# Layer 0 of a two-layer graph attention block: v and combination by ordinary products, the full-size sets by seven products

## The chip, the core and the metric

The kernel runs on one core of a Trainium2 chip. The metric is the device time of one execution in microseconds (us); the time of a kernel is the median of several executions. The core has four engines that compute: TensorE (PE in the profile) multiplies matrices and writes its results to PSUM, which here serves as eight banks of 128 partitions by 512 fp32 values; VectorE (DVE), ScalarE (ACT) and GpSimd (POOL) work element by element. Each engine takes its instructions in a fixed order, and engines wait for each other by semaphores. All data are fp32 except the adjacency mask, which is one byte per entry.

## The reference, cut to what matters

The input x holds 64 graphs of 256 nodes with 512 features, and adj a mask of 256 by 256 for each graph. Two attention layers follow each other; layer 0 has 4 heads of 64 (inner width 256), layer 1 has 8 heads of 64 (inner width 512).

```python
# layer 0
h = max(layernorm(x), 0)
q, k, v = h @ Wq, h @ Wk, h @ Wv             # 512 -> 256 each
sim = where(adj, q @ k.T / 8, -max)          # per head, 256 x 256
x = x + (softmax(sim) @ v) @ Wo + bo         # 256 -> 512, the "combination"
# layer 1
h = max(layernorm(x), 0)
h = layernorm(h) * gamma + beta
q, k, v = split(h @ w_qkv.T)                 # 512 -> 512 each
sim = where(adj | eye, q @ k.T / 8, -1e9)
x = x + (softmax(sim) @ v) @ w_out.T + b_out
```

## The kernel before

A step works on two graphs (G = 2, 512 tokens), so there are 32 steps. Layer 0 of a later step runs interleaved with layer 1 of an earlier one. The order on TensorE is written by hand: each call is placed on a time line by `at(period, place, function, ...)`, and the calls are then made in the order of their places. The order on the other engines is chosen by a scheduler when the kernel is built.

A matrix product C = A B with both factors cut into 2 by 2 blocks can be done with seven block products instead of eight, if sums of blocks are formed first and the products are added up afterwards. The kernel does so for every projection and for both combinations. A set is the seven products of one such multiplication. Each factor is kept as seven blocks (`NB = 7`): the four of the matrix, of which one is overwritten, and the sums. `PRODUCT[n]` names the weight block and the activation block that product n multiplies.

```python
NB = 7
A_OF = {(0, 0): 0, (0, 1): 1, (1, 1): 2, (1, 0): 3}
B_OF = ((0, 4, 3), (1, 3, 1))
PRODUCT = {1: (0, 0), 2: (1, 1), 3: (6, 2), 4: (2, 6), 5: (3, 3), 6: (4, 4), 7: (5, 5)}

def act_sums(b):                       # on GpSimd; b is hT, oT0 or oT1
    eng = nc.gpsimd
    eng.tensor_tensor(b[:, 5], b[:, 2], b[:, 3], ALU.subtract)
    eng.tensor_tensor(b[:, 3], b[:, 3], b[:, 0], ALU.subtract)
    eng.tensor_tensor(b[:, 4], b[:, 2], b[:, 3], ALU.subtract)
    eng.tensor_tensor(b[:, 6], b[:, 1], b[:, 4], ALU.subtract)
```

The products of a set are made in the order 1, 6, 7, 5, 2, 4, 3. Products 2, 4 and 3 are accumulated into the PSUM banks of products 1, 7 and 5, once those have been read. The pool `ps_mm` has four banks. It serves the projections, the combinations, the transposes of h and the weighted sums. The scores and the transposes of the probabilities (`sc`) have four banks of their own.

```python
def project_v(s, lyr, n):              # layer 0: width 128, 28 matmuls a step
    ...
    for t in range(NIC):               # NIC = 2 blocks of 128 tokens
        for c in range(HC):            # HC = 2 blocks of 128 features
            nc.tensor.matmul(
                bank[:, t, :], st["hT"][:, ba, c, t * P:(t + 1) * P], w[:, wa, c, 2, :], ...)
    evacuate(n, bank, token_rows(st[f"v{lyr}"], width))

def combine(s, lyr, n):                # layer 0: one chunk, 14 matmuls a step
    ...
    for t in range(NIC):
        for c in range(chunks):
            nc.tensor.matmul(
                bank[:, t, :], st[f"oT{lyr}"][:, ba, c, t * P:(t + 1) * P], w[:, wa, c, :], ...)
    accumulate(n, bank, token_rows(st["xt"], HD), st["u"])
```

`evacuate` copies products 1 and 2 on ScalarE and adds the others on VectorE. `accumulate` copies product 1 to `u` on ScalarE, adds product 6 to `u` on VectorE (L297), adds `u` to two quarters of xt on GpSimd and, after product 5, to a third; the other products are added to xt on VectorE.

A score set is 16 half-height matmuls, then per 128 rows a masked minimum on VectorE (L403) and an exponential on ScalarE (L409); a reciprocal (L414) and the scaling of the probabilities follow, half on VectorE (L419), half on ScalarE (L421). `turn` transposes the probabilities on TensorE (L430) and copies them back on both engines (L434, L436). `weigh` multiplies by v (L448), and ScalarE copies the result to oT (L454). `norm1` takes the moments of xt and of its ReLU on VectorE, makes the power -0.5 on GpSimd (L206) and the row scale on VectorE (L207); ScalarE scales the rows (L213). `mask` makes the additive mask on GpSimd (L188, and for layer 1 L192).

The order in which one step is placed, cut to the calls that matter here (p = s - 2 for layer 0, p = s for layer 1):

```python
for c in range(NC):
    at(p, 3.03 + 0.03 * c, transpose_h, s, 0, c)
at_set(p, 3.5, 1.0, project_qk, s, 0, 0)
at_set(p, 4.5, 0.5, project_v, s, 0)
at(p, 4.5, scores, s, 0, 0)
...
at_set(p, 9.0, 0.5, combine, s, 0)     # 9.0 is 3.0 of a later period
for t in range(NT):
    at(p, 9.5 + 0.25 * t, norm1, s, t)
...
at(p, 3.0, scores, s, 1, 1)
at(p, 3.75, scores, s, 1, 3)
at(p, 4.499, weigh, s, 1, 3, False, True)
at_set(p, 5.0, 1.0, combine, s, 1)
```

Of the kernel before, what the change touches and what calls it, by code (L numbers as in the profile page):

```python
# [8 lines left out]
FP = mybir.dt.float32  # L9
U8 = mybir.dt.uint8  # L10
AF = mybir.ActivationFunctionType
ALU = mybir.AluOpType
# [7 lines left out]
def kernel(  # L20
# [16 lines left out]
    nc = tc.nc  # L37
    P = 128
# [43 lines left out]

    NB = 7
    A_OF = {(0, 0): 0, (0, 1): 1, (1, 1): 2, (1, 0): 3}
    B_OF = ((0, 4, 3), (1, 3, 1))
    PRODUCT = {1: (0, 0), 2: (1, 1), 3: (6, 2), 4: (2, 6), 5: (3, 3), 6: (4, 4), 7: (5, 5)}

    def weight_sums(eng, w):
# [4 lines left out]

    def act_sums(b):
        eng = nc.gpsimd
        eng.tensor_tensor(b[:, 5], b[:, 2], b[:, 3], ALU.subtract)
        eng.tensor_tensor(b[:, 3], b[:, 3], b[:, 0], ALU.subtract)  # L97
        eng.tensor_tensor(b[:, 4], b[:, 2], b[:, 3], ALU.subtract)  # L98
        eng.tensor_tensor(b[:, 6], b[:, 1], b[:, 4], ALU.subtract)


    H0, H1, HD = I0 // 2, I1 // 2, D // 2
    HC, HP0, HP1 = NC // 2, PR0 // 2, PR1 // 2
    wqkv0 = const.tile([P, NB, HC, 3, H0], FP, name="wqkv0")
    wo0 = const.tile([P, NB, HP0, HD], FP, name="wo0")
    wqkv1 = const.tile([P, NB, HC, 3, H1], FP, name="wqkv1")
    wo1 = const.tile([P, NB, HP1, HD], FP, name="wo1")
    bo_b = const.tile([P, D], FP, name="bo_b")
# [2 lines left out]

    def first_weights():
        for (i, j), n in A_OF.items():
            for k, w in enumerate((wq, wk, wv)):
                nc.scalar.dma_start(
                    wqkv0[:, n, :, k, :],
                    w[j * D // 2:(j + 1) * D // 2, i * H0:(i + 1) * H0]
                    .rearrange("(c p) o -> p c o", p=P),
                )
        for (i, j), n in A_OF.items():  # L120
            nc.scalar.dma_start(
                wo0[:, n],
                wo[j * I0 // 2:(j + 1) * I0 // 2, i * HD:(i + 1) * HD]
                .rearrange("(c p) o -> p c o", p=P),
            )
        weight_sums(nc.vector, wqkv0)
        weight_sums(nc.gpsimd, wo0)
        for v, t in ((bo, bo_b), (b_out, bout_b)):
            nc.scalar.dma_start(t, bass.AP(tensor=v.tensor, offset=v.offset, ap=[[0, P], [1, D]]))

# [115 lines left out]
            row_scales(s, ve)  # L246


    def blocks_of(b, pairs):
        return b.rearrange("p n (c t) -> p n c t", c=pairs)  # L250

    def transpose_h(s, lyr, c):
        st = S[s]
        if c == 0:
            st["hT"] = act.tile([P, NB, HC, N], FP, name="hT")
        ph = ps_mm.tile([P, G, N], FP, name="mm")
        pv = ph.rearrange("p g n -> p (g n)")
        for t in range(NT):
            nc.tensor.transpose(pv[:, t * P:(t + 1) * P], st["h"][:, t, c * P:(c + 1) * P], ident)  # L259
        b0, b1, step = B_OF[c // HC]  # L260
        dst = st["hT"][:, b0:b1:step, c % HC, :]
        if lyr == 0:
            nc.scalar.activation(dst, ph, AF.Relu)
        else:
            nc.vector.tensor_scalar(
                dst, ph, gb[:, 0, c:c + 1], gb[:, 1, c:c + 1], op0=ALU.mult, op1=ALU.add
            )
        if c == NC - 1:
            act_sums(st["hT"])
# [50 lines left out]
    def project_qk(s, lyr, a, n):  # L320

        st = S[s]
        half, w = (PR0, PR1)[lyr] // 2, (wqkv0, wqkv1)[lyr]
        if n == 1:
            for pr in (a, a + half):
                st["qk", lyr, pr] = sm.tile([P, 2, T], FP, name="qk", bufs=3)
        t0, t1 = st["qk", lyr, a], st["qk", lyr, a + half]
        bank, first = bank_of(st, ("qk", a), n, N)
        wa, ba = PRODUCT[n]
        for k in range(2):  # L330
            for c in range(HC):
                nc.tensor.matmul(  # L332
                    bank[:, k, :], w[:, wa, c, k, a * P:(a + 1) * P], st["hT"][:, ba, c, :],
                    start=first and (k, c) == (0, 0), stop=(k, c) == (1, HC - 1),
                    skip_group_check=True,
                )
        evacuate(n, bank, (t0[:, :, :N], t0[:, :, N:], t1[:, :, :N], t1[:, :, N:]))
# [4 lines left out]
            for i in range(2) for j in range(2)  # L342
        ]

    def project_v(s, lyr, n):
        st = S[s]
        width, w = (H0, H1)[lyr], (wqkv0, wqkv1)[lyr]
        if n == 1:
            st[f"v{lyr}"] = act.tile([P, NT, 2 * width], FP, name=f"v{lyr}")
        bank, first = bank_of(st, "v", n, width)  # L350
        wa, ba = PRODUCT[n]
        for t in range(NIC):
            for c in range(HC):
                nc.tensor.matmul(  # L354
                    bank[:, t, :], st["hT"][:, ba, c, t * P:(t + 1) * P], w[:, wa, c, 2, :],
                    start=first and (t, c) == (0, 0), stop=(t, c) == (NIC - 1, HC - 1),
                    skip_group_check=True,
                )
        evacuate(n, bank, token_rows(st[f"v{lyr}"], width))

    def combine(s, lyr, n):
        st, chunks, w = S[s], (HP0, HP1)[lyr], (wo0, wo1)[lyr]
        if n == 1:
            st["u"] = sm.tile([P, NIC, HD], FP, name="u", bufs=1)
        bank, first = bank_of(st, "c", n, HD)
        wa, ba = PRODUCT[n]
        for t in range(NIC):
            for c in range(chunks):
                nc.tensor.matmul(  # L369
                    bank[:, t, :], st[f"oT{lyr}"][:, ba, c, t * P:(t + 1) * P], w[:, wa, c, :],  # L370
                    start=first and (t, c) == (0, 0), stop=(t, c) == (NIC - 1, chunks - 1),
                    skip_group_check=True,
                )
        accumulate(n, bank, token_rows(st["xt"], HD), st["u"])
# [62 lines left out]

    def weigh(s, lyr, pr, first, last):
        st, pT = S[s], S[s].pop(("pm", lyr, pr))
        half = (HP0, HP1)[lyr]  # L440
        if first:
            st[f"oT{lyr}"] = act.tile([P, NB, half, N], FP, name=f"oT{lyr}")
        po = ps_mm.tile([P, G, N], FP, name="mm")
        for g in range(G):
            for jc in range(NIC):
                for e in range(2):
# [3 lines left out]
                        st[f"v{lyr}"][:, g * NIC + jc, c0:c0 + DH],  # L450
                        pT[g, e][:, jc, :], start=(jc == 0), stop=(jc == NIC - 1),
                    )
        b0, b1, step = B_OF[pr // half]
        nc.scalar.copy(st[f"oT{lyr}"][:, b0:b1:step, pr % half, :], po)  # L454
        if last:
            act_sums(st[f"oT{lyr}"])

# [14 lines left out]
    for s in range(NSTEP):  # L474
# [7 lines left out]
        for c in range(NC):  # L482
            at(p, 3.03 + 0.03 * c, transpose_h, s, 0, c)
        at_set(p, 3.5, 1.0, project_qk, s, 0, 0)
        at_set(p, 4.5, 0.5, project_v, s, 0)
        at(p, 4.5, scores, s, 0, 0)
        at(p, 5.15, turn, s, 0, 0)
        at(p, 5.6, scores, s, 0, 1)
# [2 lines left out]
        at(p, 7.001, weigh, s, 0, 1, False, True)  # L491
        at(p, 7.4, load_x, s)
        at(p, 8.6, first_bias, s)
        at_set(p, 9.0, 0.5, combine, s, 0)
        for t in range(NT):
            at(p, 9.5 + 0.25 * t, norm1, s, t)
            at(p, 10.5 + 0.1 * t, scale_row, s, t)
# [3 lines left out]
            at(p, -0.85 + 0.15 * c, transpose_h, s, 1, c)  # L501
        at(p, 0.3, mask, s, 1)
        at_set(p, 0.0, 1.0, project_qk, s, 1, 0)
        at_set(p, 1.0, 1.0, project_v, s, 1)
        at_set(p, 2.0, 1.0, project_qk, s, 1, 1)
        at(p, 1.0, scores, s, 1, 0)
        at(p, 1.65, turn, s, 1, 0)
# [7 lines left out]
        at(p, 3.751, weigh, s, 1, 1, False, False)  # L515
        at(p, 4.25, turn, s, 1, 3)
        at(p, 4.499, weigh, s, 1, 3, False, True)
        at_set(p, 5.0, 1.0, combine, s, 1)
        at(p, 6.0, store, s)

    at(-3, 5.6, first_weights)
# [37 lines left out]
```

## Time and profile before

| what | value |
|---|---|
| time, median of 3 | 3909.32 us (3905.31 to 3909.89) |
| span of the profiled execution | 3907.4 us |
| TensorE busy | 3656.7 us, 94% |
| VectorE busy | 2410.3 us, 62% |
| ScalarE busy | 1940.0 us, 50% |
| GpSimd busy | 1379.9 us, 35% |
| HBM traffic | 29 GB/s over the span |
| distance of the layer-0 combinations of two steps that follow each other | 118.9 us |

The profile's page gives the busy time of each engine, the costliest groups of instructions (by source line, engine and tile) and the idle time before them with what ended it. The names are those of the program: `mm` is a bank of the pool `ps_mm`, `sc` a bank of the scores, `xt` the rows of x, `hT` and `oT` the transposed activations and attention outputs. Line numbers are those of the kernel before. An fp32 matmul appears as two matmul instructions, a transpose as one. The ends of matmuls are modelled, so the distance of starts is the surer measure. TensorE's loading of weights runs beside its matmuls.

### The profile page before, as it was taken

The numbers are of one execution on the slowest core, as the hardware profiler recorded it, in microseconds if no ns is written. First come the engines' busy times: TensorE is split into PE (matmuls) and PEld (weight loads), VectorE is DVE, ScalarE is ACT, GpSimd is POOL, SyncE is SP. The second block draws the span as 40 slices with busy tenths as digits, with TensorE's granted clock in tenths as the row PEclk, the third lists the DMA queues.
The fourth block names the chain that finished last, engine by engine and source line by source line (L and its number), as shares of the span: only waits on it lengthen the run. The fifth ranks groups of instructions, "written<-read, shape, count | busy, mean of one in ns | idle before, by whom it ended". The sixth has DMA issues, their size and how long they took to land. (4 is left out here: it accounts for less than half of the span.)

```text
span 3907.4 us, 59075 instructions
## 1 busy us (share of the span) xinstructions
PE 3656.7 (94%) x21953; PEld 3044.9 (78%) x21953; DVE 2410.3 (62%) x7001; ACT 1940.0 (50%) x5329; POOL 1379.9 (35%) x1170
## 2 busy tenths in 40 slices
PE   5999999999999999999999999999999999999988
PEld 4787778877777877778777878777787778787766
DVE  5566665666565666656665656666566656566654
ACT  3555554455554555544555455545455554554543
POOL 5234333343333343333433333433334333244331
PEclk9999999999999999999999999999999999999999
DMA  3011000110011110001100100100011001010000
GB/s 119 12 34 35 13 24 33 34 35 25 12 35 33 35 34 13 24 33 35 34 24 13 34 33 35 35 13 24 33 35 34 24 12 35 33 34 33 1 22 22
DMA packets 74128, 115.46 MB, mean 30 GB/s; under 512 B 18792, under 2 KB 22384, under 8 KB 73840
## 3 DMA queue, kind: packets, MB, share of 16 engines
q1 hardware_dynamic: 67584, 104.87, 8.1%
q10 hardware_dynamic: 6256, 6.82, 0.6%
q8 instruction: 172, 2.82, 0.3%
q14 instruction: 116, 0.95, 0.1%
HBM read 78.12 MB, written 33.55 MB: 29 GB/s over the span
## 5 line engine op out<-in xcount | busy, mean ns | idle before, releaser
L332 PE MATMUL mm<-hT,wqkv 128*128 128x256 f32 x5376 | 1214.0, 381 | 10.8 <-POOL hT L98 10.3
L332 PEld LDWEIGHTS mm<-hT,wqkv 128*128 128x128 f32 x5376 | 1009.2, 191 | 167.5 <-issue 24.6
L409 ACT ACTIVATE pm<-pm,sa 128x256 f32<-128x256 f32 x1536 | 758.9, 496 | 367.6 <-DVE sa L403 367.5
L403 DVE CUSTOM_DVE_ANT_0 pm<-sc,n 128x256 f32<-128x256 f32 x1536 | 553.7, 417 | 259.4 <-PE sc L393 256.8
L354 PE MATMUL mm<-wqkv,hT 128*128 128x128 f32 (+1 forms) x3584 | 639.0, 334 | 58.3 <-DVE v L280 58.3
L369 PE MATMUL mm<-wo,oT 128*128 128x256 f32 x2688 | 667.9, 399 | 19.4 <-POOL oT L98 17.9
L354 PEld LDWEIGHTS mm<-wqkv,hT 128*128 128x128 f32 x3584 | 550.3, 194 | 141.8 <-DVE v L280 64.2
L369 PEld LDWEIGHTS mm<-wo,oT 128*128 128x128 f32 x2688 | 521.5, 202 | 111.0 <-POOL oT L98 19.0
L298 POOL TENSOR_TENSOR xt<-xt,u 128x512 f32<-128x512 f32 x64 | 81.5, 1274 | 1233.7 <-DVE u L297 1233.7
L419 DVE TENSOR_SCALAR pm<-pm,sa 128x256 f32<-128x256 f32 x768 | 415.4, 582 | 5.7
L448 PE MATMUL mm<-pm,v 128*64 128x256 f32 x3072 | 374.8, 386 | 28.3 <-DVE pm L434 28.3
L393 PE MATMUL sc<-qk 64*128 64x256 f32 x3072 | 385.9, 390 | 0.3 <-DVE pm L434 0.3
L421 ACT ACTIVATE pm<-pm,sa 128x256 f32<-128x256 f32 x768 | 345.1, 497 | 73.9 <-DVE sa L414 73.9
L436 ACT COPY pm<-sc 128x512 f32<-128x512 f32 x384 | 217.9, 583 | 328.4 <-PE sc L430 328.3
L430 PE MATMUL sc<-ident,pm 128*128 128x128 f32 x3072 | 370.8, 274 | 8.9 <-DVE pm L419 8.7
L430 PEld LDWEIGHTS sc<-ident,pm 128*128 128x128 f32 x3072 | 347.9, 142 | 27.9 <-DVE pm L419 11.1
L393 PEld LDWEIGHTS sc<-qk 64*128 64x128 f32 x3072 | 282.3, 187 | 79.8 <-issue 49.0
L448 PEld LDWEIGHTS mm<-pm,v 128*64 128x64 f32 x3072 | 203.9, 137 | 177.1 <-issue 43.8
L434 DVE COPY pm<-sc 128x512 f32<-128x512 f32 x384 | 254.3, 682 | 108.9 <-PE sc L430 108.8
L213 ACT ACTIVATE h<-h,mr,r 128x512 f32<-128x512 f32 x256 | 191.1, 805 | 204.7 <-DVE mr L207 204.7
L409 ACT ACTIVATION_READ_ACCUMULATOR pm<-pm,sa 128x1 f32 x1536 | 288.4, 188 | 0.0
L259 PE MATMUL mm<-ident,h 128*128 128x128 f32 x1024 | 166.1, 301 | 117.1 <-DVE u L297 95.7
(80 smaller groups left out, 3402.7 us busy)
## 6 DMA issues: line engine op xcount, KB each, us to landing
h<-in_x_dram SPq DMA_DIRECT2D x32, 1024.0 KB, 5.3
xt<-in_x_dram SPq DMA_DIRECT2D x32, 1024.0 KB, 5.1
out_dram<-xt SPq DMA_DIRECT2D x32, 1024.0 KB, 4.3
ad<-in_adj_dram SPq DMA_DIRECT2D x32, 128.0 KB, 2.2
wr<-in_L_gnn_w_qkv_dram ACTq DMA_DIRECT2D x3, 1024.0 KB, 7.8
wr<-in_L_gnn_w_out_dram ACTq DMA_DIRECT2D x1, 1024.0 KB, 9.8
wqkv<-in_L_gnn_Wq_dram ACTq DMA_DIRECT2D x4, 128.0 KB, 5.2
wqkv<-in_L_gnn_Wk_dram ACTq DMA_DIRECT2D x4, 128.0 KB, 4.1
```

Source lines behind the costliest of these rows:

```text
L332: nc.tensor.matmul(bank[:, k, :], w[:, wa, c, k, a * P:(a + 1) * P], st["hT"][:, ba, c, :], start=first and (k, c) == (0, 0), stop=(k, c) ...
L354: nc.tensor.matmul(bank[:, t, :], st["hT"][:, ba, c, t * P:(t + 1) * P], w[:, wa, c, 2, :], start=first and (t, c) == (0, 0), stop=(t, c) ...
L369: nc.tensor.matmul(bank[:, t, :], st[f"oT{lyr}"][:, ba, c, t * P:(t + 1) * P], w[:, wa, c, :], start=first and (t, c) == (0, 0), stop=(t, ...
L393: nc.tensor.matmul(sc[g, e][:, ic, :], qk[rows, 0, i0:i0 + P], qk[rows, 1, g * N:(g + 1) * N], start=True, stop=True,)
L403: nc.vector.tensor_tensor_reduce(out=pm[g, e][:, ic, :], in0=sc[g, e][:, ic, :], in1=neg[:, g * NIC + ic, :], scale=-SCALE, scalar=SMAX, o ...
L409: nc.scalar.activation(pm[g, e][:, ic, :], pm[g, e][:, ic, :], AF.Exp, bias=sa[:, 0, g, e, ic:ic + 1], scale=-1.0, accum_out=sa[:, 1, g, e ...
L419: nc.vector.tensor_scalar(pv, pv, inv, None, op0=ALU.mult)
L421: nc.scalar.activation(pv, pv, AF.Copy, scale=inv)
L430: nc.tensor.transpose(pp[:, jc, ic * P:(ic + 1) * P], pm[:, ic, jc * P:(jc + 1) * P], ident)
L434: nc.vector.tensor_copy(pm, pp)
L436: nc.scalar.copy(pm, pp)
L448: nc.tensor.matmul(po[e * DH:(e + 1) * DH, g, :], st[f"v{lyr}"][:, g * NIC + jc, c0:c0 + DH], pT[g, e][:, jc, :], start=(jc == 0), stop=(j ...
```

## The change

The v projection and the combination of layer 0 have an inner width of 256, so that cutting them in two leaves blocks of 128. The change does these two by ordinary products: v in four blocks of 128 tokens, each an accumulation over the four feature blocks with 256 columns; the combination in four blocks of 128 tokens, each an accumulation over the two blocks of the inner width with 512 columns. The other sets, q and k of both layers, v and combination of layer 1, stay with seven products. The purpose is to have fewer and wider matmuls and fewer emptying operations in the two small sets.

```diff
-    B_OF = ((0, 4, 3), (1, 3, 1))
+    B_OF = ((0, 8, 7), (1, 3, 1))
@@ act_sums
-        eng.tensor_tensor(b[:, 5], b[:, 2], b[:, 3], ALU.subtract)
-        eng.tensor_tensor(b[:, 3], b[:, 3], b[:, 0], ALU.subtract)
+        eng.tensor_tensor(b[:, 3], b[:, 7], b[:, 0], ALU.subtract)
         eng.tensor_tensor(b[:, 4], b[:, 2], b[:, 3], ALU.subtract)
+        eng.tensor_tensor(b[:, 5], b[:, 2], b[:, 7], ALU.subtract)
         eng.tensor_tensor(b[:, 6], b[:, 1], b[:, 4], ALU.subtract)
@@ project_v is split in project_v1 (layer 1, as before) and
+    def project_v0(s, t):
+        ...
+        bank = ps_mm.tile([P, I0], FP, name="mm")
+        for c in range(NC):
+            b0, _, step = B_OF[c // HC]
+            i = t % NIC * P
+            nc.tensor.matmul(
+                bank, st["hT"][:, b0 + t // NIC * step, c % HC, i:i + P], wv0[:, c, :],
+                start=(c == 0), stop=(c == NC - 1),
+            )
+        nc.scalar.copy(st["v0"][:, t, :], bank)
@@ combine is split in combine1 (layer 1, as before) and
+    def combine0(s, t):
+        st = S[s]
+        bank = ps_mm.tile([P, D], FP, name="mm")
+        for pr in range(PR0):
+            nc.tensor.matmul(
+                bank, st["oT0"][:, pr, t * P:(t + 1) * P], wo0[:, pr, :],
+                start=(pr == 0), stop=(pr == PR0 - 1),
+            )
+        nc.vector.tensor_tensor(st["xt"][:, t, :], bank, st["xt"][:, t, :], ALU.add)
@@ weigh: layer 0 keeps oT0 whole and makes no sums of it
+        if lyr == 0:
+            if first:
+                st["oT0"] = act.tile([P, PR0, T], FP, name="oT0")
+            nc.scalar.copy(st["oT0"][:, pr, :], po.rearrange("p g n -> p (g n)"))
+            return
@@ order
-        at_set(p, 4.5, 0.5, project_v, s, 0)
+        for t in range(NT):
+            at(p, 4.5 + 0.14 * t, project_v0, s, t)
-        at_set(p, 9.0, 0.5, combine, s, 0)
+        for t in range(NT):
+            at(p, 9.0 + 0.12 * t, combine0, s, t)
-        at_set(p, 5.0, 1.0, combine, s, 1)
+        at_set(p, 5.1, 0.9, combine1, s)
```

The blocks hT and oT1 get an eighth part, so that all four blocks of the matrix stay readable beside the sums: the ordinary v products read blocks 0, 1, 2 and 7. The weights of v and of the combination of layer 0 are loaded whole, without sums. The set of products for the combination of layer 1 starts a tenth of a set later than before.

## The prediction

> **What bounds the kernel now.** First the page's busy times: TensorE is busy for 94% of the span, VectorE for 62%, so the end is set by TensorE's work plus its waits.
>
> ```profile
> PE 3656.7 (94%) x21953; PEld 3044.9 (78%) x21953; DVE 2410.3 (62%) x7001; ACT 1940.0 (50%) x5329; POOL 1379.9 (35%) x1170
> ```
>
> Second, what TensorE waits for (total, times, longest, in us):
>
> ```profile
> PE mm L259 <- DVE u L297: 95.7, 30, 3.2
> PE mm L354 <- DVE v L280: 58.3, 31, 1.9
> PE mm L448 <- DVE pm L434: 28.3, 30, 1.0
> ```
>
> Two of the three come once per step and belong to the sets that the change rewrites: L354 is the v set, and L259 (transposes of h) waits inside the layer-0 combination for a PSUM bank that L297 empties. Third, the order in time of TensorE, around the v set and around the combination (start, length, instructions; a product of fp32 is two instructions, a transpose one; the bracket is idle time before the row):
>
> ```profile
> 2012.06 1.16 PE L354 MATMUL mm<-wqkv,hT 128*128 128x128 f32 x8
> 2013.15 2.00 PE L393 MATMUL sc<-qk 64*128 64x256 f32 x16
> 2015.08 3.84 PE L354 MATMUL mm<-wqkv,hT 128*128 128x128 f32 x32
> 2020.82 2.05 PE L354 MATMUL mm<-wqkv,hT 128*128 128x128 f32 x16 [1.91 <-DVE v L280]
> 2022.71 3.62 PE L369 MATMUL mm<-wo,oT 128*128 128x256 f32 x16
> ...
> 2095.71 1.13 PE L369 MATMUL mm<-wo,oT 128*128 128x256 f32 x4
> 2096.68 1.04 PE L259 MATMUL mm<-ident,h 128*128 128x128 f32 x8
> 2097.55 1.03 PE L369 MATMUL mm<-wo,oT 128*128 128x256 f32 x4
> 2101.78 1.97 PE L259 MATMUL mm<-ident,h 128*128 128x128 f32 x8 [3.19 <-DVE u L297]
> 2103.53 5.29 PE L369 MATMUL mm<-wo,oT 128*128 128x256 f32 x20
> 2108.66 1.91 PE L430 MATMUL sc<-ident,pm 128*128 128x128 f32 x16
> ```
>
> Prices come from start to start, not from the lengths, whose ends are modelled. In the same view a row of 16 instructions (8 products) of 256 columns starts at 2088.36 and the next row at 2091.91: 0.444 us a product. The 16 instructions (8 products) of 128 columns at 2020.82 take 1.89 us: 0.236 a product. The sixteen transposes at 2108.66 take 1.75 to the next row: 0.109 each. Fourth, why the bank comes late, from the order in time of VectorE, ScalarE and GpSimd:
>
> ```profile
> 2097.94 0.61 DVE L419 TENSOR_SCALAR pm<-pm,sa 128x256 f32<-128x256 f32 x2
> 2100.51 0.62 DVE L419 TENSOR_SCALAR pm<-pm,sa 128x256 f32<-128x256 f32 x2
> 2101.04 0.68 DVE L297 TENSOR_TENSOR u<-mm,u 128x512 f32<-128x512 f32 x1
> ...
> 2100.16 0.56 ACT L295 COPY u<-mm 128x512 f32<-128x512 f32 x1
> ...
> 2121.67 2.70 DVE L419 TENSOR_SCALAR pm<-pm,sa 128x256 f32<-128x256 f32 x2
> ...
> 2120.44 2.50 POOL L192 TENSOR_TENSOR n<-n,offdiag 128x512 f32<-128x512 f32 x2
> ```
>
> Product 6 cannot be added to u before ScalarE has copied product 1 to u, and that copy stands behind eight exponentials. Both emptying engines run a softmax just then. So the stall is a queue, not arithmetic.
>
> [...] 0.236 us for 128 columns is more than half of 0.444. [...] the 3.19 us above is what a late evacuation costs. [...] the scaling pair takes 0.61 us alone and 2.70 beside L192.
>
> **The change part by part.** The order of the changed kernel's instructions on each engine is fixed before it runs, and I read it beside the durations above.
>
> *v.* Out go 7 products of 4 matmuls of 128 columns, in come 4 token blocks of 4 matmuls of 256. Columns rise from 3584 to 4096. Before, the set takes 2012.06 to 2022.71 less the scores from 2013.15 to 2015.08: 10.65 - 1.93 = 8.72 us, 1.91 of it waiting. After: 16 x 0.444 = 7.1 us. ScalarE empties block 0 before the softmax and block 1 behind the eighth exponential. In the window before, that comes about 7.4 us after the scores start. Scores and three blocks take 1.93 + 12 x 0.444 = 7.3, so the next product finds a bank. I take **-1.6 us** a step.
>
> *Combination.* Out go 14 matmuls of 256 columns with 16 transposes among them; 14 x 0.444 + 1.75 = 8.0 us of work occupy 2095.71 to 2108.66 = 12.95. In come 4 rows of 2 matmuls of 512 columns. No row has that width; twice 0.444 is 0.888, a line through 0.236 and 0.444 gives 0.860. I take 0.87 as an estimate. Clock from the first of them, by the fixed order: row 0 to 1.74; three transposed blocks to 3.05, which fills the four banks. Row 1 waits for row 0's add, which stands on VectorE behind the first scaling pair (ends at 2098.55 = 2.84) and takes 0.69: it starts at 3.5, ends at 5.25. Fourth block to 5.7. Row 2 needs the second block's bank, which ScalarE empties behind exponential 8 (2100.16 = 4.45), one ReLU (0.6), two scalings (0.9) and its own ReLU (0.5): starts at 6.45, ends at 8.2. Row 3 ends at 9.95. So 12.95 becomes 9.95: **-3.0 us**. Two waits stay, 0.5 and 0.75.
>
> *Beside the path.* GpSimd loses three 1.27-us additions of u and four 0.73-us sums of oT0 a step, VectorE five additions of v, ScalarE gains little. The sums of hT are reordered, so that block 4, which product 6 reads, is second instead of third: 1.3 us earlier.
>
> *A new wait.* VectorE now has the scale of the second normalization (L207 before) inside the last layer-1 softmax, ahead of a scaling pair and of product 7's addition to q and k. It waits for GpSimd's power, placed behind the mask of the next step, which in turn waits for that softmax's last reduction. From the durations (mask 1.08, power 1.02, then the two L192 beside the pair), VectorE loses some 2 us waiting [...]. Product 4 needs that addition, so it starts 1.9 to 3.2 us late; but 0.95 us of an old wait after it (L448 on L434) is swallowed, and some transposes' copies come no later. Against the old place of that weighing I get +0.8 to +2.0; I take **+1.3 us**.
>
> Sum: -1.6 - 3.0 + 1.3 = -3.3 us a step, 30 steady steps: -99. In the first two steps TensorE waits 12.22 us once on the sums of oT0 and 3 us twice on those of hT, with GpSimd busy throughout. It loses about 2.9 + 2.5 us of work there and the right block comes 1.3 earlier: about -8. Total -107: 3909 - 107 = 3802.
>
> **The rivals.** (1) *The waits stay and only the columns count.* Then v costs 7.1 against 6.8 without its wait (+0.3) and the combination 8 x 0.87 against 14 x 0.444 (+0.7): 32 steps, +32, about 3941. For it: both emptying engines are still in a softmax. Against it: the new rows need no u, and the adds stand between softmax parts in the fixed order. (2) *No new wait.* Then -4.6 a step: 3909 - 138 - 12 = 3759. For it: VectorE has 38% idle. Against it: its queue is in order and its wait for GpSimd is explicit. (3) *The new wait is larger*, the pair blocked by both masks and the copies late: +2.9, thus -1.7 a step, about 3850. (4) *Hidden transfer*: the row loads land at about 2056 and are added to the bias by 2062, while the combination starts at 2095; a period 3 us shorter does not reach them.
>
> **Range and chances.** The range goes from nearly rival 2 to rival 3: 3765 to 3850. Faster by over 2% means below 3831, that is 2.3 us a step with the start-up as assumed. Only the pessimistic end misses that: 0.78. Within 2%: 0.19. Slower would need rival 1 and the new wait together: 0.03.
>
> **What would show it.** Right: the v set without idle time, 7.1 us; combination 10 us from first row to the transposes of pm, with two waits under 1 us; 512-column products at 0.87; the wait on u at L297 about zero in layer 0; a VectorE wait of about 2 us on the power, and a TensorE wait of 2 to 3 us in front of a layer-0 product of q and k. Wrong: 512-column products well above 0.89; waits of 3 us still in front of row 1; or the new wait absent or above 4 us, which moves the total by 40 us or more either way.

## The result, and the profile after

The changed kernel takes 3854.68 us (median; 3853.67 to 3856.24) against 3907.45 us of the kernel before in the same measurement. The ratio is 0.9865 with a 95% interval of 0.9848 to 0.9882: 53 us or 1.3% faster, where 107 us had been predicted, and a little outside the predicted range. The distance between the layer-0 combinations of neighbouring steps (called the period from here on; mean of 29) fell from 119.43 to 118.18 us, by 1.25 us and not by 3.3 (the 118.9 us in the table of before is the distance of one pair).

In the profile of the changed kernel, first the page's busy times:

```profile
PE 3680.3 (95%) x20801; PEld 2936.7 (76%) x20801; DVE 2301.6 (60%) x6777; ACT 1941.8 (50%) x5361; POOL 1141.5 (30%) x942
```

and then what TensorE waits for (total, times, longest, in us):

```profile
PE mm L325 <- DVE qk L273: 99.3, 30, 3.3
```

TensorE has 1152 instructions fewer and is busy 24 us longer: the ordinary products stream more columns (8192 instead of 7168 in the two sets of a step). Time at half clock, which comes up below, counts as busy in both kernels. The three waits of before, 182 us together, are gone. In their place stands a new one, 3.3 us in each step, before a product of q and k of layer 0 (L325), and two small ones in the new combination.

Next the order in time of TensorE in the changed kernel (start, length, instructions, idle time before the row): the combination, the q, k set behind it with the turn (L446), and the v set (L346). The weighing (L461), ahead of which the kernel before waits 0.95 us, follows at 2099.75.

```profile
2064.95 1.98 PE L371 MATMUL mm<-wo,oT 128*128 128x512 f32 x4
...
2068.44 1.98 PE L371 MATMUL mm<-wo,oT 128*128 128x512 f32 x4 [0.20 <-DVE xt L375]
...
2071.31 3.70 PE L371 MATMUL mm<-wo,oT 128*128 128x512 f32 x8 [0.45 <-ACT hT L256]
2074.85 1.91 PE L446 MATMUL sc<-ident,pm 128*128 128x128 f32 x16
...
2092.71 2.44 PE L325 MATMUL mm<-hT,wqk 128*128 128x256 f32 x8 [3.31 <-DVE qk L273]
2094.94 3.15 PE L446 MATMUL sc<-ident,pm 128*128 128x128 f32 x16
2097.93 1.89 PE L325 MATMUL mm<-hT,wqk 128*128 128x256 f32 x8
...
2101.63 1.99 PE L346 MATMUL mm<-wv,hT 128*128 128x256 f32 x8
2103.55 2.00 PE L409 MATMUL sc<-qk 64*128 64x256 f32 x16
...
2110.76 1.89 PE L385 MATMUL mm<-wo,oT 128*128 128x256 f32 x8
```

The combination goes from 2064.95 to 2074.85, 9.90 us. Eight instructions (four products) of 512 columns take 3.54 us from 2071.31 to the next row, 0.885 a product. The v set, 2101.63 to 2110.76 less 1.93 for the scores inside it, takes 7.2 us without idle time. The two rows after the new wait are the surprise: a row of 16 transposes takes 3.0 us to the next start at 2094.94, and 1.74 at 2074.85. The view by stretches of time shows why. Its columns are the stretch, its length, the busy time of PE, PEld, DVE, ACT and POOL with their instructions, and then the granted clock of TensorE (1.00 is full).

```profile
2094.90:2098.00 3.10, 3.10 (x18) 3.06 (x17) 1.69 (x3) 0.59 (x1) 0.00 (x0) 0.59 0.00 0
2098.00:2100.00 2.00, 2.00 (x11) 1.46 (x12) 0.53 (x2) 0.59 (x1) 0.00 (x0) 1.00 0.00 0
```

After the idle 3.31 us TensorE runs at half clock for a while: the granted clock in the trace is 0.50 from 2094.06 to 2097.47 us and 1.00 on both sides of it. The same view of the kernel before, around its idle 3.19 us in the combination, shows the same (0.50 from 2101.75 to 2105.16), and nothing in the prediction counts with it:

```profile
2101.80:2105.20 3.40, 3.40 (x12) 3.08 (x13) 0.00 (x0) 1.89 (x4) 3.25 (x3) 0.51 0.00 0
```

The page hides this: in its row of forty slices the clock has the digit 9 throughout.

Where the new wait comes from is in the order in time of VectorE in the changed kernel,

```profile
2085.96 1.02 DVE L241 TENSOR_TENSOR ve<-ve,mg 128x4 f32<-128x4 f32 x1
2088.11 1.22 DVE L203 SCALAR_TENSOR_TENSOR mr<-mg,r 128x4 f32<-128x4 f32 x1 [1.14 <-POOL r L202]
...
2089.45 2.51 DVE L435 TENSOR_SCALAR pm<-pm,sa 128x256 f32<-128x256 f32 x2
2091.89 0.68 DVE L273 TENSOR_TENSOR qk<-mm,qk 128x512 f32<-128x512 f32 x1
```

and in that of GpSimd over the same time:

```profile
2085.92 1.05 POOL L184 TENSOR_SCALAR n<-ad 128x1024 f32<-128x1024 uint8 x1 [2.09 <-DVE mg L195]
2087.06 1.02 POOL L202 TENSOR_TENSOR r<-ve,mhalf 128x4 f32<-128x4 f32 x1
2088.05 2.49 POOL L188 TENSOR_TENSOR n<-n,offdiag 128x512 f32<-128x512 f32 x2
```

The operations on 128 x 4 elements, L241 and L203, take 1.02 and 1.22 us beside a GpSimd operation; alone they take 0.16 (shown below). Between them VectorE waits 1.14 us for the power r, which GpSimd makes after the mask (L184) from the result of L241; the mask and L241 end at the same moment, at about 2086.98. The scaling pair takes 2.51 us beside L188. Only then comes the addition L273 that TensorE waits for.

### The profile page after: what moved, and what is told of

It reads as the page before. It is cut to its first block, busy times and chain, and to the rows that moved or that the text cites. A ratio compares the mean times of both kernels' runs of the same rounds, so it can differ in the third digit from the quotient of the medians.

```text
span 3853.8 us, 56369 instructions
## 1 busy us (share of the span) xinstructions
PE 3680.3 (95%) x20801; PEld 2936.7 (76%) x20801; DVE 2301.6 (60%) x6777; ACT 1941.8 (50%) x5361; POOL 1141.5 (30%) x942
## 4 chain that ended last, share of the span: by engine, by line
PE 75%; DVE 12%; ACT 10%; POOL 1%; issue 1%; DMA 0%; POOLq 0%; DVEq 0%
PE mm L325 24%; PE mm L360 10%; PE mm L385 10%; PE mm L461 8%; PE sc L446 8%; PE sc L409 7%; PE mm L346 6%; ACT pm L425 5%; DVE pm L435 3%; DVE bs L194 2%; ACT h L235 2%; PE mm L252 2%; ACT pm L437 1%; ACT hT L256 1%; DVE xt L375 1%
## 5 line engine op out<-in xcount | busy, mean ns | idle before, releaser
L325 PE MATMUL mm<-hT,wqkv 128*128 128x256 f32 x3584 | 803.4, 380 | 1.4 <-POOL hT L97 1.4
L325 PEld LDWEIGHTS mm<-hT,wqkv 128*128 128x128 f32 x3584 | 673.2, 190 | 102.0 <-issue 12.3
L325 PE MATMUL mm<-hT,wqk 128*128 128x256 f32 x1792 | 433.9, 396 | 111.2 <-DVE qk L273 99.3
L325 PEld LDWEIGHTS mm<-hT,wqk 128*128 128x128 f32 x1792 | 341.9, 196 | 179.2 <-POOL oT L96 110.4
L96 POOL TENSOR_TENSOR hT<-hT 128x512 f32<-128x512 f32 x64 | 81.5, 1273 | 1252.9 <-ACT hT L256 1237.9
L385 PE MATMUL mm<-wo,oT 128*128 128x256 f32 x1792 | 417.6, 382 | 0.2 <-POOL oT L97 0.2
L360 PE MATMUL mm<-wqkv,hT 128*128 128x256 f32 x1792 | 405.8, 381 | 0.0
L446 PEld LDWEIGHTS sc<-ident,pm 128*128 128x128 f32 x3072 | 365.9, 147 | 44.7 <-issue 19.8
L446 PE MATMUL sc<-ident,pm 128*128 128x128 f32 x3072 | 387.3, 281 | 8.9 <-DVE pm L435 8.8
L360 PEld LDWEIGHTS mm<-wqkv,hT 128*128 128x128 f32 x1792 | 335.3, 190 | 55.2 <-issue 12.3
L461 PE MATMUL mm<-pm,v 128*64 128x256 f32 x3072 | 375.8, 387 | 0.0
L385 PEld LDWEIGHTS mm<-wo,oT 128*128 128x128 f32 x1792 | 331.6, 191 | 53.3 <-issue 12.7
L435 DVE TENSOR_SCALAR pm<-pm,sa 128x256 f32<-128x256 f32 x768 | 354.2, 503 | 4.6
L461 PEld LDWEIGHTS mm<-pm,v 128*64 128x64 f32 x3072 | 204.3, 137 | 147.2 <-issue 54.5
```

What stands on the lines that cost most here:

```text
L325: nc.tensor.matmul(bank[:, k, :], w[:, wa, c, k, a * P:(a + 1) * P], st["hT"][:, ba, c, :], start=first and (k, c) == (0, 0), stop=(k, c) ...
L360: nc.tensor.matmul(bank[:, t, :], st["hT"][:, ba, c, t * P:(t + 1) * P], wqkv1[:, wa, c, 2, :], start=first and (t, c) == (0, 0), stop=(t, ...
L385: nc.tensor.matmul(bank[:, t, :], st["oT1"][:, ba, c, t * P:(t + 1) * P], wo1[:, wa, c, :], start=first and (t, c) == (0, 0), stop=(t, c) ...
L435: nc.vector.tensor_scalar(pv, pv, inv, None, op0=ALU.mult)
L446: nc.tensor.transpose(pp[:, jc, ic * P:(ic + 1) * P], pm[:, ic, jc * P:(jc + 1) * P], ident)
L461: nc.tensor.matmul(po[e * DH:(e + 1) * DH, g, :], st[f"v{lyr}"][:, g * NIC + jc, c0:c0 + DH], pT[g, e][:, jc, :], start=(jc == 0), stop=(j ...
```

## The experiments

Theory, from the two traces: the two rewritten sets gained what was predicted, and the gain came back in the q, k set, by a wait that GpSimd's mask makes and by half a clock after that wait. Rivals: one of the two parts does not gain; the clock is an effect of something else; or the wait is made by something other than the mask. All kernels were measured beside the kernel before. A period given below is the usual one, which most steps of the profiled execution have, unless it is called a mean; for the kernel before it is 119.2 us.

### One part alone

Only v by ordinary products; the combination again with seven:

```diff
-        for t in range(NT):
-            at(p, 9.0 + 0.12 * t, combine0, s, t)
+        at_set(p, 9.0, 0.5, combine, s, 0)      # with wo0 as blocks and sums, u, sums of oT0
```

> Only v of layer 0 by ordinary products; its combination stays with seven products. Theory A (the gains of the two parts are real and separate, 1.5 us a step for v and 3.05 for the combination, and what eats them comes with the combination, because its early rows move the second normalization on VectorE into the last layer-1 softmax): the v set shows no wait, the 3.2 us wait in the combination stays, there is no wait of TensorE in front of a layer-0 product of q and k, and the time is 3907 - 31 x 1.5 - 3 = about 3858. Theory B (the new wait comes with any of the two parts, VectorE being short of time): a wait of 2 to 3 us in the q and k set here too, time about 3900 or more.

Only the combination by ordinary products; v again with seven:

```diff
-        for t in range(NT):
-            at(p, 4.5 + 0.14 * t, project_v0, s, t)
+        at_set(p, 4.5, 0.5, project_v, s, 0)
```

> Only the combination of layer 0 by ordinary products; v stays with seven products. Theory A: the combination takes 9.9 us instead of 12.95, the v set keeps its 1.9 us wait, and the q and k set shows the 3.3 us wait on VectorE together with half-clock stretches; the gain of 3.05 a step is eaten by about 2.5 + 1.0, the start saves some 15 us: about 3900. Theory B: the wait is there but smaller, since VectorE also has v's additions elsewhere; 3880 or less.

Measured: v alone 3801.13 us, ratio 0.9724 (0.971 to 0.9739), 54 us better than both parts together and 57 us below the 3858 of theory A. The combination alone 3889.27 us, ratio 0.9949 (0.9934 to 0.9964), 11 us below the 3900 of theory A. In the trace with v alone, TensorE has the 3.19 us of idle time in the combination as before, but nothing slow behind it:

```profile
2043.91 1.09 PE L258 MATMUL mm<-ident,h 128*128 128x128 f32 x8 [3.19 <-DVE u L296]
2044.84 4.49 PE L381 MATMUL mm<-wo,oT 128*128 128x256 f32 x20
```

The transposes take 0.93 us to the next row, where the kernel before took 1.75, and the products 4.33 where it took 5.13: 1.62 us less for the same instructions. With the v set's own 1.5 us that gives 3.1 of the 3.2 us by which the period fell, from 119.2 to 116.04. So v is not worth 3 us: half of it is the clock. In the trace with the combination alone, the opposite: the new wait is there (99.2 us in 30), and the half clock is longer.

```profile
2104.98 3.75 PE L323 MATMUL mm<-hT,wqk 128*128 128x256 f32 x8 [3.30 <-DVE qk L271]
2108.53 2.97 PE L431 MATMUL sc<-ident,pm 128*128 128x128 f32 x16
```

To the starts of the next rows these take 3.55 and 2.80 us; at full clock 1.80 and 1.75. That is 2.8 us lost behind the wait, in a period of 119.47 us. The wait belongs to the combination, not to v: its earlier rows bring the second normalisation forward into the q, k set. One part of the expectation failed: with v by seven products again, the old 1.9 us wait on v is not there.

### The idle stretch filled

The changed kernel with six products by zero weights, which add nothing, in front of the place where TensorE waits:

```diff
+        if lyr == 0 and n == 2:
+            for i in range(6):
+                nc.tensor.matmul(bank[:, 0, :], zero, st["hT"][:, ba, 0, :],
+                                 start=False, stop=False, skip_group_check=True)
```

> The changed kernel with six further matmuls of 256 columns by a weight tile of zeros, added to product 2's bank in the layer-0 q and k set, just where TensorE then idles 3.3 us (6 x 0.444 = 2.7 us of work that adds zero). Theory C (an idle stretch of 3.3 us makes the clock drop to half for some 3 us in 18 of 29 steps, 1.67 us each): the filled kernel does more work and is faster, 3855 - 18 x 1.67 = about 3825, all periods 117.1 us long. Rival (the stretched matmuls and transposes after the wait are themselves waits for VectorE or ScalarE): no gain, 3855 or a little more.

Measured: 3828.65 us, ratio 0.9794 (0.9779 to 0.9808); all 29 periods 117.14 to 117.16 us. More work on the busiest engine makes the kernel 26 us faster. The wait that is left is 0.7 us and nothing is slow behind it; the mean granted clock of the profiled run is 0.995, where the changed kernel has 0.987. In the kernel without filler, 11 of 29 periods have 117.14 us and 18 have 118.81: the 11 are those without half clock, and the filler makes all of them so.

The kernel before, with five such products in its combination, and then with seven of 128 columns in its v set too:

```diff
+        for i in range(5 if (lyr, n) == (0, 6) else 0):       # in combine
+            nc.tensor.matmul(bank[:, 0, :], zero, w[:, 0, 0, :],
+                             start=(i == 0), stop=False, skip_group_check=True)
+        for i in range(7 if (lyr, n) == (0, 6) else 0):       # in project_v, second run only
+            nc.tensor.matmul(bank[:, 0, :], zero, w[:, 0, 0, 2, :],
+                             start=(i == 0), stop=False, skip_group_check=True)
```

> The kernel before, with five further matmuls of 256 columns by a weight tile of zeros put at the head of product 6 in the layer-0 combination, where TensorE then idles 3.2 us (5 x 0.444 = 2.2 us of work that adds zero). Theory C' (in the kernel before, too, that idle stretch halves the clock for the stretch after it: its eight transposes take 1.75 us and not 0.87, its ten matmuls 5.1 and not 4.4, and the kernel with v alone changed, whose combination has the same idle stretch and no slow stretch, is 1.6 us a step faster there): the kernel with useless work added is faster, 3909 - 30 x 1.6 = about 3860. Rival (the slow stretch in the kernel before is a second wait for banks): no gain, 3909.

> The kernel before with its two long idle stretches of TensorE filled by products with zero weights: 5 of 256 columns in the combination of layer 0 (the 3.2 us wait on u), and 7 of 128 columns ahead of product 6 of layer 0's v (the 1.9 us wait on v). With the first filler alone the period stayed 119.5 us, and its trace shows why: the 16 instructions after the 1.9 us wait on v then took 3.20 us instead of 2.05, at a granted clock of 0.59. Theory A (an idle stretch of TensorE can be followed by about 3 us of half clock, and each such stretch costs 1.2 to 1.6 us; with both filled none is left): 1.3 us less in 29 periods, about 3870 us, period 118.1 us, mean clock 0.995. Rival B (the half clock comes back at whatever short wait is next, for example the 0.95 us one before the weighing): again 3906 us.

Measured: 3906.44 us with the first filler, ratio 0.9992 (0.9983 to 1.0001), the miss of this series. The combination became shorter (12.95 to 11.66 us) and had no slow row, yet the period stayed. The stretches of that run say where it went. The two rows are the 1.9 us wait on v and what follows it:

```profile
2133.00:2135.00 2.00, 0.12 (x1) 0.12 (x2) 1.79 (x4) 1.66 (x6) 1.92 (x2) 1.00 0.00 0
2135.00:2138.00 3.00, 3.00 (x17) 3.00 (x18) 1.48 (x5) 1.16 (x3) 0.16 (x1) 0.59 0.00 0
```

Here 1.9 us of idle time is followed by half a clock, as in 23 of this run's 26 steps between 400 and 3500 us. With the second filler that is gone, and the mean clock is 0.993: 3895.75 us, ratio 0.9963 (0.995 to 0.9975), period 118.95. This is less than the 3870 expected, because that filler was mostly extra work. Its 14 instructions took 1.67 us to the next start, and the wait on v behind them fell only from 1.91 to 1.42, so the v set became 1.1 us longer. With that, 119.2 (the usual period before) - 1.3 + 1.1 = 119.0 is what was measured.

### What decides about the half clock

Two kernels with the same idle stretch in the same place, one nearly always without half clock (v alone) and one always with it (before), can't be told apart by the stretch. So the kernel with v alone was given one, and three, products of zero weights in a set of layer 1 where nothing waits. The expectations put them at 0.47 and 1.42 us a step; in the trace the periods without half clock grow from 116.04 to 116.47 and to about 117.33 us, by 0.43 and 1.3.

```diff
+        if (lyr, a, n) == (1, 0, 2):                           # in project_qk
+            for i in range(1):                                 # 3 in the second run
+                nc.tensor.matmul(bank[:, 0, :], zero, st["hT"][:, ba, 0, :],
+                                 start=False, stop=False, skip_group_check=True)
```

> Only v by ordinary products (as in the run with 3801 us), plus one product of 256 columns with zero weights (two instructions, 0.47 us) in layer 1's first q, k set of each step, far from any wait. That run had 3.19 us of idle TensorE in each combination and yet no half clock after it, with a period of 116.04 us; other kernels with the same idle stretch had it in all or some periods. Theory A (whether the idle stretch halves the clock depends on when it falls against something that runs by itself, so that another period moves the phase): some or all of the 29 periods are now 1.6 us longer than 116.5, with the row of 8 transposes at 2 us in place of 1.1; 3815 to 3865 us. Rival B (it depends on the idle stretch and the work around it alone, which are unchanged): every period 116.5 us, no half clock, 3815 us.

> The same with three such products (1.42 us a step). Theory A: periods of 117.5 and of 119.1 us, a mixture or one of the two, and by the share of periods with half clock another than with one product; 3843 to 3890 us. Rival B: every period 117.45 us, 3843 us.

Measured: 3879.61 us with one product (ratio 0.9925, 0.991 to 0.9939) and 3875.06 with three (0.9917, 0.99 to 0.9933). A single product of 0.43 us in a step, 14 us in all, made the kernel 78 us slower than v alone; one product costs more than three. That is beyond what theory A gave for the first (3865), because behind many stretches the half clock lasts twice as long there and costs up to 3.0 us. The rows of one such step in the first run, and the stretch of half clock (by the columns given above), which begins 1.1 us before the first of them:

```profile
2315.53 1.97 PE L260 MATMUL mm<-ident,h 128*128 128x128 f32 x8 [3.19 <-DVE u L298]
2317.30 6.44 PE L389 MATMUL mm<-wo,oT 128*128 128x256 f32 x20
```

```profile
2314.40:2321.20 6.80, 5.67 (x18) 4.86 (x19) 2.01 (x5) 3.04 (x7) 5.57 (x5) 0.50 0.00 0
```

The traces record the granted clock, 1.00 or 0.50, and when it changes. Between 400 and 3500 us all 62 changes of the kernel before, and all 32 of the changed kernel, lie at multiples of 3.4133 us from one point of the run, to 0.001 us. These points are called boundaries here, counted on where the clock does not change (in the other runs by the same spacing), and the 3.413 us between two of them an interval. A half-clock stretch lasts one interval, 3.41 us (all 31 of the kernel before and all 16 of the changed one), or, in some steps of other runs, two, 6.83 us. Take for every step the time from the last boundary to the start of the idle stretch (its phase), beside it the time from the stretch's end to the first row of the next group, and the length of the half clock:

```text
kernel           start after a boundary       time behind     half clock   steps
three products   1.82 to 2.19                 5.25 to 5.27    none           7
three products   2.27 to 3.40, 0.06 to 0.10   6.92 to 6.95    3.41          19
changed kernel   1.49 to 1.97                 5.37            none          10
changed kernel   2.15 to 3.04                 7.04 to 7.05    3.41          16
v alone          1.76 to 2.06                 5.25 to 5.27    none          26
v alone          0.65                         6.69            3.41           1
before           2.61 to 3.37, 0.12 to 0.82   6.61 to 6.94    3.41          26
one product      1.84                         5.26            none           1
one product      2.26 to 2.64, 0.91 to 0.92   6.55 to 6.94    3.41           9
one product      0.94 to 1.33                 8.04 to 8.24    6.83          16
```

Phase alone divides these 131 steps, without an exception. A stretch of 3.2 to 3.3 us that starts 1.5 to 2.1 us after a boundary (one of 3.19 us up to 2.2) is cut by the next boundary into two parts of less than 2 us, and no half clock follows; in all the others one interval holds more than 2.0 us of it. (In these rows the half clock lasts for a second interval where the stretch goes on for 0.72 to 1.11 us beyond the boundary at which the half clock begins, and for one only where it goes on for 0.70 us or less.) The 1.9 us wait on v fits: in the kernel before and in that with the first filler, half clock follows where it starts 0.11 to 1.44 us after a boundary and so lies inside one interval (28 steps), and not where it starts at 1.46 us or later (24). My estimate from these 131 and 52 steps is that about 2 us of idle time inside one interval are enough; no stretch in the table fills an interval. The steps with one interval at half clock lose 1.66 to 1.69 us where the whole interval falls on work, about half of 3.413. The kernel with v alone has a period of 116.04 us = 34.0 intervals, so each step has nearly the same phase, a harmless one. The combination alone has the opposite luck: 119.47 us = 35.0 intervals, and two intervals at half clock in 24 of its 26 steps. What in the chip sets the interval, the traces don't show.

### The mask moved

The changed kernel with layer 1's mask made to depend on a later result, so that GpSimd takes it after the power r and not before. In the first run it depends on the last scaled row of h, in the second on r itself:

```diff
+            big = stat.tile([P, 1], FP, name="big", bufs=2)
+            nc.gpsimd.tensor_scalar(big, S[s]["h"][:, NT - 1, :1], 0.0, BIG, ...)  # second run: S[s]["r"][:, :1]
-            nc.gpsimd.tensor_scalar(n, S[s]["ad"], -1.0, BIG, op0=ALU.add, op1=ALU.mult)
+            nc.gpsimd.tensor_scalar(n, S[s]["ad"], -1.0, big, op0=ALU.add, op1=ALU.mult)
```

> The changed kernel, with the additive mask of layer 1 made to depend on the last scaled row of h, so that on GpSimd it comes after the power and not before it; one GpSimd instruction of 128x1 a step is added, nothing else differs. Theory A (VectorE waits about 1.1 us for the power behind the mask, [...]): the wait in front of product 4 falls from 3.3 to about 1 us or less, the clock no longer drops, 2.5 + 1.0 us a step: about 3750 to 3775. Rival (VectorE simply has too much work in that stretch): the wait stays near 3 us, 3850.

> The changed kernel, with the additive mask of layer 1 made to depend on the power, so that on GpSimd it comes directly after the power: VectorE no longer waits for the mask, but the mask's three instructions still run beside the scaling pair. If the wait for the power is the larger part, P4's wait falls from 3.3 to about 1.5 us or less and the clock keeps up: about 3760 to 3780. [...] the wait stays at 2 to 3 us: 3790 to 3830, depending on whether the clock drops.

Measured: 3735.9 us, ratio 0.9556 (0.954 to 0.9572), and 3731.41 us, ratio 0.9549 (0.9534 to 0.9563). Both are below what was expected, by 14 and 29 us. (The first expectation counted, beside the wait, on the three operations of VectorE that are slow beside the mask: 1.02 + 1.22 + 2.51 us above.) The periods are 114.35 and 114.19, and TensorE's wait on the q, k addition is 0.5 and 0.4 us. VectorE in the second run:

```profile
2018.15 0.16 DVE L245 TENSOR_TENSOR ve<-ve,mg 128x4 f32<-128x4 f32 x1
2019.45 0.16 DVE L207 SCALAR_TENSOR_TENSOR mr<-mg,r 128x4 f32<-128x4 f32 x1 [1.13 <-POOL r L206]
...
2019.73 1.48 DVE L439 TENSOR_SCALAR pm<-pm,sa 128x256 f32<-128x256 f32 x2
2021.14 0.67 DVE L277 TENSOR_TENSOR qk<-mm,qk 128x512 f32<-128x512 f32 x1
```

The wait for r is the same, 1.13 us. The two small operations take 0.16 instead of 1.02 and 1.22, and the pair 1.48 instead of 2.51. From the start of the one to the addition it is 2.99 us instead of 5.93. These three operations account for the whole 2.94 us: it was the collision, that is VectorE's operations taking longer beside GpSimd's, and not the wait for r, that the mask's old place cost. VectorE and ScalarE make the same operations in the same order in a step of all three kernels; only GpSimd's order differs. By its times alone the second expectation would give the other reading. It took the pair's part of the collision to stay beside the mask, with 3790 to 3830 us if that was the larger part, but the move ended most of that too: of the pair's 1.9 us some 0.9 is left. The trace shows the price: in the changed kernel the two operations on 128 x 4 elements end with the GpSimd instruction beside them, after 1.02 us (L184, 1.05 us) and 1.22 us (the first L188, 1.27 us). By what the one engine holds up the other was not shown.

Is the mask's place a matter of this change, or of any of these kernels? The same edit on the kernel before, and on the kernel with the combination alone:

> The kernel before with only the mask of layer 1 made to depend on the power r of the second normalisation, so that GpSimd takes it after r and not 11 us ahead of it. Theory A (the mask costs time only where the change has brought the second normalisation forward into the q, k set of layer 0, next to it): the kernel before has no wait on the q, k additions and its mask lies away from the power, so nothing to win: 3895 to 3925 us, period within 0.5 us of 119.4. Rival B (the place of the mask is worth its 1.6 to 4 us a step in any kernel, and has nothing to do with the change): 3830 us or less.

> Only the combination by ordinary products (v of layer 0 still by seven), and the mask of layer 1 made to depend on the power r of the second normalisation, so that GpSimd takes it after r. Without the second edit this kernel had 3889 us, a wait of 3.3 us on the q, k additions of layer 0 and 1.8 us of half clock after it in every period of 119.47 us. Theory A (the combination's 3.05 us are real, and only the mask on GpSimd gave them back by way of that wait): the wait falls to about 0.4 us, the clock stays at 1, and what is left is 119.4 - 3.05 + 0.4 = 116.8 us a period, about 3810 us with the earlier start; up to 1.3 us more (3850) if half a clock comes after the 1.9 us wait on v that may return. Rival B (the combination's gain is only nominal, or the period is held by something else): 3885 us or more.

Measured: the kernel before with the edit 3810.24 us, ratio 0.9746 (0.973 to 0.9762). The expectation that it wins nothing fell. In that kernel the mask lay beside the scaling pair ahead of the weighing of layer 1 (2.70 us, shown in the prediction). With the edit the pair takes 0.62 us. In the wait table the 28 us of the weighing are gone, the wait on v falls from 58.3 to 43.6 us, and the one on u stays at 95.7; but that idle stretch now falls into a harmless phase (usual period 116.03 us, 34.0 intervals; the stretch starts 1.42 to 2.11 us after a boundary in 25 of 27 steps, and the transposes behind it take 0.93 us). So the edit wins 100 us in the kernel before and 123 in the changed one, but in different ways. In the changed kernel 2.94 of 3.99 us a step are the collision at the place to which the change brought the normalization, and 1.04 the half clock behind it. In the kernel before, of 3.2 us a step about 1.9 are half clock that no longer comes (1.62 in the combination, 0.28 at v), the larger part by phase alone, and about 1.4 are shorter waits.

The combination alone, with the edit: 3718.15 us, ratio 0.9509 (0.9495 to 0.9524), the fastest kernel of all, period 113.71. Theory A had given 3810. It missed because the wait on v did not return, and because the 0.95 us wait of the weighing was gone too, which it had left in. (The 1.8 us of half clock in that expectation is the loss on the first row alone; both rows lose 2.8.) The v set of this kernel:

```profile
2022.46 1.16 PE L350 MATMUL mm<-wqk,hT 128*128 128x128 f32 x8
...
2025.48 5.81 PE L350 MATMUL mm<-wqk,hT 128*128 128x128 f32 x48
2031.12 1.89 PE L375 MATMUL mm<-wo,oT 128*128 128x256 f32 x8
```

Seven products of v take 2022.46 to 2031.12 less 1.93 for the scores, 6.7 us without idle time; the ordinary ones take 7.2. So once the wait is gone, v by ordinary products costs 0.5 us a step, which is the difference of the two periods (114.19 and 113.71). Why the wait on v goes when the combination changes was not tried by itself. The trace offers this: before, VectorE's scaling pair inside the v set took 1.63 us beside a sum of oT on GpSimd; in the fastest kernel GpSimd is done by then, and the pair takes 0.61.

## Why the prediction was wrong, by its own steps

**v, -1.6 a step: right in size.** 8.72 to 7.2 us is 1.5, and the set has no idle time. But the gain is the wait alone, and that wait goes by itself when the combination is changed; in the end the step is worth +0.5.

**Combination, -3.0: right in size.** 9.90 us against 9.95 predicted, with waits of 0.20 and 0.45 us against 0.5 and 0.75, and 0.885 us for a product against 0.87. One reason given for it was incomplete: "the stall is a queue" holds for 3.19 us, but 1.6 of the 12.95 us were products and transposes at half clock.

**The new wait, +1.3: the step that failed.** Its place was right, its size was not. From the turn's start to the weighing the kernel before takes 20.7 us (2108.66, shown in the prediction, to 2129.36):

```profile
2129.36 1.95 PE L448 MATMUL mm<-pm,v 128*64 128x256 f32 x16 [0.95 <-DVE pm L434]
```

The changed kernel, in a period without half clock, takes 23.24:

```profile
302.69 1.91 PE L446 MATMUL sc<-ident,pm 128*128 128x128 f32 x16
...
325.93 1.95 PE L461 MATMUL mm<-pm,v 128*64 128x256 f32 x16
```

That is +2.54, above the upper end of +2.0. The prediction had VectorE wait 2 us for the power behind the mask and took the scaling pair to be up to 2.1 us longer beside the mask, from its 2.70 against 0.61 us. It waits 1.14, and as long with the mask moved (1.13), so this wait is not the mask's. It loses 1.9 on the pair, as the prediction allowed, and another 1.9 on two operations of four columns (0.16 to 1.02 and 1.22), which the prediction does not name. Then the prediction took off more than the 0.95 us of old wait that the new one swallows: 3.31 - 0.95 is 2.36 already, and I had chosen +1.3 within a range that did not hold it.

**What no step had: the clock.** The new wait of 3.31 us was followed by half clock where its phase was 2.15 to 3.04 us, and not at 1.49 to 1.97. In 18 of 29 periods that costs 1.67 us, 1.04 in the mean. The kernel before had paid the same kind of sum in its combination in nearly every period, and at v in five of them, so there it was counted as part of "-3.0".

**The sum.** Against -3.3 predicted, -1.5 - 3.05 + 2.54 + 1.04 = -0.97 us, and the half clock at v that five periods of before had (119.2 to 120.84 us; 0.28 in the mean) makes -1.25, the difference of the measured means. Over 29 periods that is 36 us. **Start, -8:** the second combination begins at 174.01 us instead of 184.68, 10.7 us earlier, and from the start of the combination 29 periods later to the end it is 252.6 us instead of 259.2. 36 + 10.7 + 6.6 = 53 us, as measured.

**The rivals.** Rival 3 (+2.9, about 3850) was nearest, with part of the cause it gave (the pair blocked) and without the clock. Rival 1 was wrong: its waits went. Rival 2, no new wait, is what the mask edit brought about, and there the time is 3731, even below its 3759.

What the change is worth by itself depends on what stands beside it. Without half clock, the period would be about 117.56 us before (the usual 119.2 less 1.64) and is 117.14 after: 0.4 us. With the mask out of the way, where neither kernel has half clock in its usual period, it is 116.03 against 114.19, and 113.71 for the combination alone.

## What to carry to other kernels

In these runs a wait had a second price where half clock followed it (by my estimate, from about 2 us inside one interval of 3.413 us; mostly 1.68 us a time): look at the granted clock in the 3 us behind each repeated wait before putting a size on it, and when two versions differ by 1 or 2% see first whether their clocks differ. When a change moves an operation of one engine to a new place, list what GpSimd does beside it, and allow for even the smallest VectorE operation there the length of GpSimd's instruction (here 0.16 us became 1.02 beside one of 1.05, and 1.22 beside one of 1.27). Judge two changes in one kernel by both alone and together: here their gains did not add, and the better kernel has only one of them, with a mask that GpSimd makes behind the power and not ahead of it.

## What the runs showed of the hardware that was not expected

- The granted clock changed only at multiples of 3.413 us from one point (62 times in the kernel before and 32 in the changed one, between 400 and 3500 us), and the same idle stretch of 3.19 us was followed by half clock or not by its phase against them: not where it started 1.42 to 2.19 us after a boundary, always from 2.26 on and up to 1.39. The half clock lasted one interval or two and cost mostly 1.68 us, and up to 3.0.
- A kernel whose period was near a whole number of intervals (116.04 us, 34.0, or 119.47 us, 35.0) stayed at one phase for nearly its whole run, a good one in the first case and a bad one in the second; 0.43 us more work in a step of the first then made 78 us of difference.
- Products by zero weights, put into a wait of 3.3 us, kept the clock up (0.995 in the mean, against 0.987) and made the changed kernel 26 us faster.
- An idle stretch of 1.9 us was followed by half a clock as well, where it lay inside one interval (28 steps of 52).
- A VectorE operation on 128 x 4 elements took 0.16 us alone, and 1.02 to 1.22 us beside GpSimd.
